# Gated cross-attention and expert layer on one core: scores on array quarters, and five reorderings of the work around them

## The chip, the cores and the metric

The kernel runs on one core of a Trainium2 chip. TensorE multiplies matrices into PSUM, VectorE (DVE), ScalarE (ACT) and GpSimd (POOL) do the rest, SyncE (SP) issues most transfers. The metric is the time of one execution in device microseconds. Before the change it is 368.51 us, the median of 6 runs that lie between 365.48 and 370.79.

## The reference, cut to what matters

All is float32. 8 sequences of 256 tokens with 128 features; the context has 1601 positions, of which the causal mask lets only the first 256 be seen. 16 heads of 64. Then each token goes through one of 8 experts (128 to 512 to 128).

```python
def attention(queries, keys, values, mask, Wq, bq, Wk, bk, Wv, bv, Wo, bo):
    q, k, v = ...                                    # 16 heads of 64
    scores = einsum('bhqd,bhkd->bhqk', q, k) / sqrt(64)
    scores = where(mask[:, None, None, :], -1e30, scores)
    scores = where(triu(ones((256, 1601)), k=1), -1e30, scores)
    out = softmax(scores) @ v
    return out @ Wo + bo

def experts(x, W1, b1, W2, b2, Wr, br):
    indices = argmax(softmax(x @ Wr + br))
    out = 0
    for i in range(8):                               # b1, b2 are added for every token
        mask = (indices == i)[..., None]
        h = relu((x * mask) @ W1[i] + b1[i])
        out = out + (h @ W2[i] + b2[i])
    return out

x = x + tanh(g_xattn) * attention(layernorm(x), ctx, ctx, mask, ...)
x = x + tanh(g_ffn) * experts(layernorm(x), ...)
```

A token whose visible keys are all masked attends to all 1601 positions alike; the kernel carries this case by a separate mean over the context (`ksum`, `mean_value`) and a weight `umask`. An expert that a token doesn't choose still adds `relu(b1) @ W2 + b2`; the sum of these over the experts is `total`.

## The kernel before, in words

Sequences are taken in 4 pairs (`p`), heads in 8 pairs (`c`); one turn of the main loop is one `g = 8 p + c`, 32 turns. The order on every engine is that of the program text (`manual_schedule`), so an instruction that waits holds all that stands behind it on its engine.

In turn `g` the text has, in this order: `turn(old, 0..3)`, which transposes the normalized probabilities of turn `old = g - 2` on TensorE and copies them to SBUF on VectorE (`probT`, two PSUM buffers), with `query(g + 1)`, `key(g + 1)`, `value(g + 2)` and the second half of the exps of turn `g - 1` between them; `normalized(g - 1)`, in which VectorE takes reciprocals and GpSimd multiplies the probabilities by them; work for other pairs (`beside_copies`, `beside_values`, `beside_scores`: normalization, transposes, output projection `y`, router); then `biases(g)` and `scores(g, b)` with `exps(g, 0)`, and `values(old)`. `query`, `key`, `value`, `values`, `y` and small products share the two PSUM buffers of `misc`.

`biases` writes mask and causal mask of the first 128 queries (t = 0) into the score banks by a bf16 product with the identity, 4 matmuls of 128x128 by 130 columns. `scores` adds the products of t = 0 (128 keys) and writes those of t = 1 (256 keys), for the two heads j = 0, 1 of the pair: K = 64 rows, so j sits in the upper or lower row half of the array. VectorE takes the maxima, for t = 1 together with the mask. Each bank tile `banks[b]` has one PSUM bank for each j.

Beside this, GpSimd issues five accumulating 1 MB loads and a short one (`add_keys`, L148 and L150) at the end of turns 0 to 5, each into the same tile; `join_keys` (L351) adds the halves of it at the end of turn 7; `mean_value` on TensorE begins with `cm_ps` (L357) after the scores of turn 8. `other(e)` and `others()` (turns 12 to 25) prepare the experts' constant, with a long VectorE sum (L335). `keep_weights` writes the experts' weights and constants to DRAM (`later`).

Tokens are routed by rows of 264 numbers that go to their expert's place in a DRAM tile `store` (`scatter`, an indirect transfer that GpSimd issues). `last_turns` does the last two head pairs' remaining work by halves of the last pair (`a`, `b`), plans on VectorE which chunks of 128 rows are already full (`plan_full`, 18 small steps), and fetches five of those (`fetch_full`: for each a number loaded to a register on SP, then the rows, then weights from `later`). `last_routing` runs these five chunks (`turned_rows`, `first_layer`, `second_layer`) while the last tokens are routed, and `experts()` the rest.

The start: loads, constants, `ln_stats` of pair 0 with its scales on GpSimd, warming matmuls (`keep_awake`), transposes, `query(0)`, `key(0)`, `mask_bias(0)`, `value(0)`, `value(1)`, routing constants, the mask biases of pairs 1 to 3, and then the loop.

Of the kernel before, what the change touches and what calls it, by code (L numbers as in the profile page):

```python
# [17 lines left out]
P = 128  # L18
B, S, D = 8, 256, 128
SK = 1601  # L20
# [21 lines left out]


# [5 lines left out]
def tile_gated_xattn_moe(  # L49
# [41 lines left out]
    def load_x(eng, p):  # L91
        eng.dma_start(
            out=x_sb[p].rearrange("p (b t) d -> p b t d", b=2),
            in_=x[2 * p : 2 * p + 2].rearrange("b (t p) d -> p b t d", p=P),
        )
# [28 lines left out]
    nc.sync.dma_start(out=mask_sb, in_=mask[:, 0:S].partition_broadcast(P))  # L124
    nc.sync.dma_start(out=wv_sb, in_=wv)

# [42 lines left out]
    causal = const.tile([P, SW], F32, name="causal")  # L169
    nc.gpsimd.memset(causal, 0.0)  # L170
    for at in (K0, K1 + P):
        nc.gpsimd.affine_select(
            out=causal[:, at : at + P],
            in_=causal[:, at : at + P],
            compare_op=ALU.is_ge,
            fill=NEG,
            base=0,
            pattern=[[-1, P]],
            channel_multiplier=1,
        )  # L180
# [5 lines left out]
    bias = const.tile([P, B, SW], BF16, name="bias")  # L186
# [14 lines left out]
    def plain_constants():  # L201
# [10 lines left out]
        nc.vector.memset(bias[:, :, 0:1], 0.0)  # L212
        nc.vector.memset(bias[:, :, U0 : U0 + 1], NEG_ALL)

        for b in range(2):
            nc.vector.memset(banks[b][:, :, U1 : U1 + 1], -NEG_ALL)

    def mask_bias(p):

        for at, n in ((K0, P), (K1, S)):  # L220
            nc.vector.scalar_tensor_tensor(
                out=bias[:, 2 * p : 2 * p + 2, at : at + n],
                in0=mask_sb[:, 2 * p : 2 * p + 2, 0:n],
                scalar=NEG,
                in1=causal[:, at : at + n].unsqueeze(1).to_broadcast([P, 2, n]),
# [46 lines left out]
    token_i, _ = counted("token", [NT], [[P, NT]], 0, 1)  # L272
# [3 lines left out]
    def routing_constants():  # L276
        nc.gpsimd.memset(before, 1.0)
# [3 lines left out]
        for i, f, pattern, base, mult in made:  # L281
            nc.gpsimd.iota(i, pattern=pattern, base=base, channel_multiplier=mult)
            nc.vector.tensor_copy(f, i)
        nc.vector.tensor_copy(rows[:, :, 2 * D : 2 * D + 1].bitcast(I32), token_i.unsqueeze(2))
# [8 lines left out]
    def experts_weights():  # L293

        nc.gpsimd.memset(blank, 0.0)
# [27 lines left out]
    def others():  # L323

        part = ws[:, :, FF + AT_C : FF + AT_C + D]
        zero = p1.tile([P, E, D], F32, tag="rest", name="zero")
        for h in range(2):
# [647 lines left out]
    def last_turns():  # L975
# [19 lines left out]
        for n in (10, 11):  # L995
            scatter(n)
            apart()
# [291 lines left out]
```

## Time and profile before

| | us |
|---|---|
| profiled execution, its own time | 367.18 |
| its span, first to last instruction | 365.5 |
| first score matmul (turn 0) | 18.45 |
| start of scores, turns 7, 8, 9 | 74.03, 81.57, 94.61 |
| start of scores, turns 20, 21, 22, 23 | 190.90, 202.81, 212.71, 220.39 |
| start of scores, turn 31 | 288.18 |
| first layer of the first chunk that `experts()` runs | 324.40 |

The groups of instructions by line, with shapes kept apart, show TensorE's parts; the columns are the busy time in us, the mean duration of one in ns, and the idle time just before them with what ended it:

```profile
L540 PE MATMUL pt<-ident,prob 128*128 128x128 f32 x384 | 63.9, 278 | 3.2 <-DVE probT L542 1.7 <-POOL prob L532 1.5
L478 PE MATMUL sc<-kT,qT 64*128 64x256 f32 x256 | 38.5, 377 | 0.0
L553 PE MATMUL o<-probT,v 128*64 128x256 f32 x240 | 37.6, 392 | 0.0
L478 PE MATMUL sc<-kT,qT 64*128 64x128 f32 x256 | 28.1, 296 | 0.0
```

An f32 matmul of the text is two instructions. The mean of one holds the way through the array, so rates are read from the starts in the timeline and not from it. `64*128` is the tile of the array: 64 rows, 128 columns.

The page's slices of the span (40 of 9.1 us) show the granted clock and the transfers:

```profile
PEclk9999999999999999999999999999999999899997
DMA  6999777768499994000000000057000016659930
```

The clock is full but for one place near 314 us and the end. SP's issues of the five early chunks in the tail:

```profile
302.06 2.10 SPq L876 DMA_DIRECT2D rows<-store  x2
304.48 0.33 SPq L886 DMA_DIRECT2D arena<-later  x1
305.65 1.46 SPq L876 DMA_DIRECT2D rows<-store  x2
307.35 0.33 SPq L886 DMA_DIRECT2D arena<-later  x1
308.53 0.34 SPq L876 DMA_DIRECT2D rows<-store  x1
309.10 1.66 SPq L886 DMA_DIRECT2D arena<-later  x3
```

### The profile page before, as it was taken

The page shows a single profiled execution, that of the slowest core. Times are in us where ns is not written, and L with a number is a line of the kernel's source. Part 1 is how long each engine was busy: PE and PEld are TensorE (multiplying, and loading weights), DVE is VectorE, ACT ScalarE, POOL GpSimd, SP SyncE. Part 2 cuts the span into 40 slices and gives each one's busy share as a digit, 9 for nine tenths or more (in the row PEclk, how much of TensorE's full clock was granted, in tenths as well). Part 3 has the DMA queues.
Part 4 walks back from the last instruction along what each step waited for, and adds up shares of the span by engine and source line. Part 5 has one row for each costly group of instructions (what it writes and reads, how often), then busy time and mean ns, then how long its engine had stood idle before and what let it go on. Part 6 is the DMA issues. An engine that isn't in the chain of part 4 may idle for free.

```text
span 365.5 us, 7926 instructions
## 1 busy us (share of the span) xinstructions
PE 342.6 (94%) x2598; PEld 246.0 (67%) x2598; DVE 241.5 (66%) x838; ACT 207.8 (57%) x743; POOL 214.5 (59%) x306
## 2 busy tenths in 40 slices
PE   8879999899999999999999899999999898689993
PEld 3345656467677776667775566777767686689993
DVE  3747777675667676786767877766667985354441
ACT  2567687563555758655575386555485532356651
POOL 4065765572456576769772567692666774417673
PEclk9999999999999999999999999999999999899997
DMA  6999777768499994000000000057000016659930
GB/s 196 288 144 208 108 115 116 169 235 227 131 388 387 383 384 169 2 2 2 3 0 17 15 16 18 2 224 311 7 24 19 0 61 189 257 157 330 406 145 13
DMA packets 36320, 53.58 MB, mean 147 GB/s; under 512 B 3801, under 2 KB 22829, under 8 KB 36280
## 3 DMA queue, kind: packets, MB, share of 16 engines
q1 hardware_dynamic: 28280, 44.07, 35.2%
q0 software_dynamic: 7360, 8.73, 12.6%
q8 instruction: 20, 0.33, 0.4%
q10 hardware_dynamic: 640, 0.29, 0.3%
q14 instruction: 20, 0.16, 0.1%
HBM read 27.82 MB, written 25.71 MB: 146 GB/s over the span
## 4 chain that ended last, share of the span: by engine, by line
PE 74%; DVE 9%; ACT 9%; issue 3%; DMA 2%; POOL 1%; POOLq 0%; SPq 0%; DVEq 0%; ACTq 0%
PE sc L478 11%; PE o L553 10%; PE pt L540 9%; PE q L438 6%; ACT prob L509 6%; PE y L592 6%; PE k L445 5%; PE hs L917 5%; PE v L456 5%; PE ys L933 5%; DVE sc L488 3%; PE y_last L710 2%; PE sc L467 2%; ACT kT L447 2%; DMA rows<-store 1%
## 5 line engine op out<-in xcount | busy, mean ns | idle before, releaser
L509 ACT ACTIVATE prob<-sc,nmax 128x129 f32<-128x129 f32 (+1 forms) x256 | 105.3, 426 | 92.2 <-DVE nmax L488 92.2
L532 POOL TENSOR_TENSOR prob<-prob,rs 128x256 f32<-128x256 f32 (+1 forms) x128 | 102.7, 861 | 63.5 <-DVE rs L523 63.3
L540 PEld LDWEIGHTS pt<-ident,prob 128*128 128x128 f32 x384 | 46.8, 141 | 54.4 <-issue 47.3
L542 DVE COPY probT<-pt 128x384 f32<-128x384 f32 x128 | 67.2, 545 | 16.3 <-PE pt L540 16.3
L540 PE MATMUL pt<-ident,prob 128*128 128x128 f32 x384 | 63.9, 278 | 3.2 <-DVE probT L542 1.7
L488 DVE CUSTOM_DVE_ANT_0 sc<-sc,bias 128x256 f32<-128x256 f32 x128 | 55.3, 432 | 4.4
L509 ACT ACTIVATION_READ_ACCUMULATOR prob<-sc,nmax 128x1 f32 x256 | 53.6, 209 | 0.0
L478 PE MATMUL sc<-kT,qT 64*128 64x128 f32 (+1 forms) x512 | 50.6, 337 | 0.0
L553 PE MATMUL o<-probT,v 128*64 128x256 f32 x480 | 45.6, 332 | 0.0
L553 PEld LDWEIGHTS o<-probT,v 128*64 128x64 f32 x480 | 29.7, 136 | 18.3 <-issue 8.0
L478 PEld LDWEIGHTS sc<-kT,qT 64*128 64x128 f32 x512 | 36.3, 187 | 4.9
L486 DVE TENSOR_REDUCE nmax<-sc 128x2 f32<-128x258 f32 x64 | 27.0, 422 | 12.3 <-PE sc L478 12.2
L438 PE MATMUL q<-xT,arena 128*128 128x512 f32 x64 | 33.2, 600 | 1.5 <-DVE xT L410 0.8
L456 PE MATMUL v<-arena,cT 128*128 128x512 f32 x64 | 33.0, 599 | 1.6 <-ACT qT L440 1.5
L445 PE MATMUL k<-cT,arena 128*128 128x512 f32 x64 | 33.5, 605 | 0.8 <-DVE total L336 0.8
L440 ACT ACTIVATE qT<-q,bqT 128x512 f32<-128x512 f32 x32 | 22.0, 688 | 13.9 <-PE q L438 13.1
L523 DVE RECIPROCAL rs<-ssum 128x4 f32<-128x4 f32 x64 | 11.0, 173 | 27.9 <-ACT prob L509 23.0
L951 POOL DMA_INDIRECT out_dram<-o,rows x18 | 17.9, 996 | 16.1 <-DMA rows<-store 8.3
L925 ACT ACTIVATE h<-hs,arena 128x128 f32<-128x128 f32 x60 | 17.2, 368 | 16.0 <-ACT h L925 8.8
L447 ACT ACTIVATE kT<-k,bT 128x512 f32<-128x512 f32 x32 | 22.2, 694 | 2.8 <-PE k L445 2.8
L569 DVE TENSOR_SCALAR arena<-o,bT 128x512 f32<-128x512 f32 x30 | 22.4, 746 | 1.2 <-PE o L553 1.2
L592 PE MATMUL y<-wo_sb,arena 128*128 128x128 f32 x192 | 23.1, 275 | 0.0
(234 smaller groups left out, 503.6 us busy)
## 6 DMA issues: line engine op xcount, KB each, us to landing
store<-blank SPq DMA_DIRECT2D x16, 1056.0 KB, 14.7
arena<-later SPq DMA_DIRECT2D x15, 578.0 KB
rows<-in_ctx_dram POOLq DMA_DIRECT2D x5, 1024.0 KB, 9.0
later<-ws SPq DMA_DIRECT2D x1, 4624.0 KB
rows<-store SPq DMA_DIRECT2D x23, 132.0 KB, 3.6
ws<-in_L_ffn_W_dram SPq DMA_DIRECT2D x1, 2048.0 KB
ws<-in_L_ffn_W_dram SPq DMA_DIRECT2D x8, 256.0 KB, 5.3
x<-in_x_dram SPq DMA_DIRECT2D x4, 256.0 KB
```

The lines of the kernel that those rows point to most:

```text
L438: nc.tensor.matmul(ps, lhsT=wq_sb[:, c * P : (c + 1) * P], rhs=xT[p], start=True, stop=True)
L445: nc.tensor.matmul(ps, lhsT=wk_sb[:, c * P : (c + 1) * P], rhs=cT[p], start=True, stop=True)
L447: nc.scalar.activation(kT[g], ps, AF.Identity, bias=bT[:, NC + c : NC + c + 1])
L456: nc.tensor.matmul(ps, lhsT=cT[p][:, t * P : (t + 1) * P], rhs=wv_sb[:, c * P : c * P + 512], start=True, stop=True)
L478: nc.tensor.matmul(s[:, j, at : at + n], lhsT=q[r, b * S + t * P : b * S + (t + 1) * P], rhs=k[r, b * S : b * S + n], start=(t == 1), stop ...
L488: nc.vector.tensor_tensor_reduce(out=s[:, j, K1:U1], in0=s[:, j, K1:U1], in1=bias[:, 2 * (g // NC) + b, K1:U1], scale=-1.0, scalar=-NEG_AL ...
L509: nc.scalar.activation(pr[:, j, lo:hi], s[:, j, lo:hi], AF.Exp, bias=m[:, t, j : j + 1], scale=-1.0 if t else 1.0, accum_out=sm[:, t, j : ...
L532: nc.gpsimd.tensor_tensor(pr[:, :, lo:hi], pr[:, :, lo:hi], r, ALU.mult)
L540: nc.tensor.transpose(ps[:, n * P : (n + 1) * P], pr[:, j, K0 + n * P : K0 + (n + 1) * P], ident)
L542: nc.vector.tensor_copy(pt, ps[:, 0 : 3 * P])
L553: nc.tensor.matmul(o[DK * j : DK * (j + 1), n * P : S], lhsT=v[:, 2 * b + n, cols], rhs=probT[g, 2 * b + j][:, 0:S] if n == 0 else probT[g ...
L592: nc.tensor.matmul(ps[:, i * D : (i + 1) * D], lhsT=attT[p * NC + c][:, t * P : (t + 1) * P], rhs=wo_sb[:, c], start=(c == 0), stop=(c == ...
```

## The change

Scores: queries of t = 1 are loaded with their two halves of 64 swapped, so that every matmul of `scores` and `biases` is 64 rows by 64 columns of the array (j selects the rows, u the columns), with only as many keys as the 64 queries of a quarter can see: 64, 128 for t = 0 and 256, 192 for t = 1. The mask tiles are built for that order; a token's number follows its row. GpSimd: layer norm scales of the next pair, `add_keys`, `add_bo`, `join_keys` and the experts' fills now stand behind `normalized` of a turn; `blank` is set at the start. The sum `total` is taken in four pieces, in eleven steps of `others()` instead of six. The first biases and scores stand ahead of the routing constants and of the second turn's projections. `router(2)`, `router_places(2)` and the scatters of the third pair stand a turn earlier, four of the first half's output products stand in turn 31, and the plan and `fetch_full` earlier in `last_turns`, with other weights between the rows.

```diff
+HB = P // 2
+BLOCK = ((0, 1), (3, 2))
...
     def load_x(eng, p):
-        eng.dma_start(
-            out=x_sb[p].rearrange("p (b t) d -> p b t d", b=2),
-            in_=x[2 * p : 2 * p + 2].rearrange("b (t p) d -> p b t d", p=P),
-        )
+        for at, t, lo in ((slice(0, P), 0, 0), (slice(0, HB), 1, P + HB), (slice(HB, P), 1, P)):
+            eng.dma_start(
+                out=x_sb[p][at, t::2],
+                in_=x[2 * p : 2 * p + 2, lo : lo + at.stop - at.start].rearrange("b q d -> q b d"),
+            )
...
     def mask_bias(p):
-        for at, n in ((K0, P), (K1, S)):
+        b = slice(2 * p, 2 * p + 2)
+        for part, out, keys, lo in (
+            (slice(0, P), bias0[0][:, b, K0:], causal0[0], 0),
+            (slice(0, P), bias0[1][:, b, K0:], causal0[1], 0),
+            (slice(0, P), bias[:, b, 0 : 3 * HB], causal1[:, 0 : 3 * HB], 0),
+            (slice(0, HB), bias[:, b, 3 * HB : S], causal1[:, 3 * HB : S], 3 * HB),
+        ):
...
     def routing_constants():
+        nc.gpsimd.memset(blank, 0.0)
...
+    def routing_casts():
...
     def experts_weights():
-        nc.gpsimd.memset(blank, 0.0)
...
         for h in range(2):
             ps = misc(f"zero_{h}")
...
-        yield
+            yield
+        for k in range(0, D, 32):
+            nc.vector.tensor_reduce(
+                total[:, k : k + 32], zero[:, :, k : k + 32].rearrange("p e d -> p d e"), AX.X, ALU.add
+            )
+            yield
...
-        nc.vector.tensor_reduce(total, zero.rearrange("p e d -> p d e"), AX.X, ALU.add)
...
     def biases(g):
         for b in range(2):
-            for j in range(2):
-                nc.tensor.matmul(
-                    banks[b][:, j, 0:K1], lhsT=ident_bf, rhs=bias[:, 2 * (g // NC) + b, 0:K1], start=True, stop=False
-                )
+            for u, keys in enumerate(bias0):
+                for j in range(2):
+                    r = slice(HB * j, HB * (j + 1))
+                    nc.tensor.matmul(
+                        banks[b][HB * u : HB * (u + 1), j, 0 : keys.shape[-1]],
+                        lhsT=ident_bf[r, r],
+                        rhs=keys[r, 2 * (g // NC) + b],
+                        start=True,
+                        stop=False,
+                    )
     def scores(g, b):
-        for at, n, t in ((K0, P, 0), (K1, S, 1)):
-            for j in range(2):
-                r = slice(DK * j, DK * (j + 1))
-                nc.tensor.matmul(
-                    s[:, j, at : at + n],
-                    lhsT=q[r, b * S + t * P : b * S + (t + 1) * P],
-                    rhs=k[r, b * S : b * S + n],
...
+        for t, at in enumerate((K0, K1)):
+            for u in range(2):
+                n = HB * (BLOCK[t][u] + 1)
+                for j in range(2):
+                    r = slice(DK * j, DK * (j + 1))
+                    lo = b * S + t * P + HB * u
+                    nc.tensor.matmul(
+                        s[HB * u : HB * (u + 1), j, at : at + n],
+                        lhsT=q[r, lo : lo + HB],
+                        rhs=k[r, b * S : b * S + n],
...
     def fetch_full():
-        weights_behind = {1: (0,), 3: (1,), 4: (2, 3, 4)}
+        weights_behind = {1: (0,), 4: (1, 2, 3, 4)}
...
-    def last_turns():
+    def last_turns(a):
-        scatter(8)
         normalized(l, 0)
+        plan(4)
         turn(g, 0)
         turn(g, 1)
         exps(l, 1)
-        scatter(9)
+        scatter(10)
         normalized(l, 1)
-        for n in (10, 11):
-            scatter(n)
-            apart()
+        scatter(11)
+        apart()
         a.residual()
-        a.out(*range(NC - 3))
-        plan(4)
+        a.out(NC - 4)
+        plan(5)
         turn(l, 0)
         turn(l, 1)
         a.attend(g, nc.scalar)
-        plan(5)
+        plan(len(steps))
+        fetch_full()
         a.out(NC - 3)
         turn(g, 2)
         turn(g, 3)
         a.attend(l, nc.scalar)
-        plan(len(steps))
-        fetch_full()
         a.out(NC - 2)
+        b.out(0)
         b.residual()
-        b.out(0)
...
         value(0)
         value(1)
+        biases(0)
+        scores(0, 0)
+        exps(0, 0)
+        scores(0, 1)
         routing_constants()
-        more_constants()
...
                 turn(old, 1)
+            if g == NG - 1:
+                o_old = misc(f"o_{old}")
+                a = Half(0, misc("y_last0")[:, 0:S], banks[0][:, 0, 0:S], banks[1][:, 0])
+                a.out(*range(NC - 4))
...
                     normalized(g - 1, b)
+            if 1 <= g < SK // S:
+                add_keys(g)
+            if g == SK // S - 1:
+                experts_weights()
+            if p + 1 < NPAIR and c == 3:
+                ln_scales(f"x{p + 1}")
+            if p < NPAIR and c == 4:
+                add_bo(p)
+            if g == NC:
+                join_keys()
+            if 2 * NC + 5 <= g < 2 * NC + 8:
+                next(rest_of)
...
-            if g < NG:
+            if g == 0:
+                beside_copies(p, c)
+                routing_casts()
+                more_constants()
+            if g > 0:
                 biases(g)
                 scores(g, 0)
...
             if g == NC:
                 next(mean)
             if old is not None:
-                values(old)
-            if g < SK // S:
+                values(old, o_old if g == NG - 1 else None)
+            if g == NG - 3:
+                router(2)
+            if g == 0:
                 add_keys(g)
-            if g == SK // S - 1:
-                experts_weights()
             if NC + 4 <= g < NC + 4 + E:
                 other(g - NC - 4)
-            if NC + 4 + E <= g < NC + 10 + E:
+            if NC + 4 + E <= g < NC + 12 + E:
                 next(rest_of)
-            if g == NC + 11 + E:
+            if g == NC + 12 + E:
                 keep_weights()
-            if p < NPAIR and c == 3:
-                add_bo(p)
-            if g == NC - 1:
-                join_keys()
             if 20 <= g < 24:
                 scatter(g - 20)
-            if 26 <= g < 30:
-                scatter(g - 22)
             if g == NG - 2:
                 residual(NPAIR - 1)
+            if 26 <= g:
+                scatter(g - 22)
```

## The prediction

> **What bounds the kernel now.** I read the page first: the busy row, then the chain of waits by engine.
>
> ```profile
> PE 342.6 (94%) x2598; PEld 246.0 (67%) x2598; DVE 241.5 (66%) x838; ACT 207.8 (57%) x743; POOL 214.5 (59%) x306
> ...
> PE 74%; DVE 9%; ACT 9%; issue 3%; DMA 2%; POOL 1%; POOLq 0%; SPq 0%; DVEq 0%; ACTq 0%
> ```
>
> TensorE is the path; the rest of it is a few stalls. Next the timeline of TensorE in one plain turn of the loop (a turn is one `g`).
>
> ```profile
> 217.24 1.03 PE L445 MATMUL k<-cT,arena 128*128 128x512 f32 x2
> 218.11 0.49 PE L540 MATMUL pt<-ident,prob 128*128 128x128 f32 x3
> 218.44 1.02 PE L456 MATMUL v<-arena,cT 128*128 128x512 f32 x2
> 219.30 0.49 PE L540 MATMUL pt<-ident,prob 128*128 128x128 f32 x3
> 219.63 0.60 PE L409 MATMUL tr_y<-ident,rows 128*128 128x128 f32 x4
> 220.06 0.39 PE L467 MATMUL sc<-bias,ident_bf 128*128 128x130 bf16 x4
> 220.39 1.58 PE L478 MATMUL sc<-kT,qT 64*128 64x128 f32 x16
> 221.90 1.52 PE L553 MATMUL o<-probT,v 128*64 128x256 f32 x16
> ```
>
> Starts follow each other without a hole: biases 0.33 us, scores 1.51, values 1.45. `k` streams 2 x 512 columns in 0.87 us, so an f32 matmul instruction costs 0.85 ns a column. The 16 score instructions hold 8x128 + 8x256 = 3072 columns, 2.61 us in single file; they take 1.51. So two row halves (j = 0, 1) already run side by side, at 1.31 us, and 0.20 us is the first weight load and the change of tile shape. Score to score is 7.6 to 7.7 us in such a turn, 9.0 to 9.5 where an output projection (`y`) stands in it.
>
> Then the three places where TensorE waits or will wait: GpSimd in turns 5 to 8, VectorE's long sum in turn 22, and the tail.
>
> ```profile
> 65.85 1.34 POOL L150 DMA_DIRECT2D rows<-in_ctx_dram  x1 [4.46 <-DMA rows<-in_ctx_dram]
> 66.69 1.05 POOL L295 MEMSET blank<- 128x528 f32 x1
> 67.80 0.13 POOL L298 MEMSET blank<- 128x1 int32 x2
> 67.90 3.16 POOL L532 TENSOR_TENSOR prob<-prob,rs 128x256 f32<-128x256 f32 x4
> 73.19 3.16 POOL L532 TENSOR_TENSOR prob<-prob,rs 128x256 f32<-128x256 f32 x4 [2.13 <-DVE rs L523]
> 76.31 2.35 POOL L351 TENSOR_TENSOR rows<-rows 128x1024 f32<-128x1024 f32 x1
> 80.75 3.16 POOL L532 TENSOR_TENSOR prob<-prob,rs 128x256 f32<-128x256 f32 x4 [2.08 <-DVE rs L523]
> ```
>
> ```profile
> 83.08 1.95 PE L357 MATMUL cm_ps<-ones,rows 128*128 128x1 f32 x16
> ```
>
> ```profile
> 207.33 1.91 DVE L335 TENSOR_REDUCE total<-zero 128x128 f32<-128x1024 f32 x1
> ```
>
> ```profile
> 313.54 0.33 PE L908 MATMUL xs<-ident,rows 128*128 128x128 f32 x1 [3.29 <-DMA rows<-store]
> 313.70 1.69 PE L917 MATMUL hs<-xsT,arena 128*128 128x128 f32 x8
> 315.37 2.05 PE L933 MATMUL ys<-arena,h 128*128 128x128 f32 x8
> 317.22 1.13 PE L917 MATMUL hs<-xsT,arena 128*128 128x128 f32 x8
> 318.18 1.06 PE L933 MATMUL ys<-arena,h 128*128 128x128 f32 x8
> ```
>
> **Scores on quarters, the largest term.** A row half streams 2 x (128+256) = 768 columns a turn, twice. In quarters, u=0 gets 64+256 and u=1 gets 128+192, so each quarter streams 640. If four run side by side: 2 x 640 x 0.85 = 1.09 us for 1.31, -0.22. Of the 0.20 us overhead, the first load has 64 columns instead of 128 (-0.05), and biases and scores share one shape, so the change of shape comes before the biases and not between. Biases: 8 matmuls for 4. Now the four cost 4 x 0.056 = 0.22 and the rest of their 0.33 is that change. With four at once there are two rounds of 0.06: -0.1; one after another +0.24. I take the first, since the row pairs start together. Sum: -0.35 us a turn; bounds -0.45 (all overhead shared) and +0.6 (only two quarters at once: 2 x 1280 columns, 2.18 us for 1.31, less 0.25 of the other savings).
>
> [...] The row: 16 one-column f32 matmuls on 128-column weights (`cm_ps`) take 1.95 us, 0.11 a load, so a plain 64-column load is 0.057 us; 14 bf16 ones (L648 to L652, 287.51 to 287.86) take 0.025 each. [...]
>
> ScalarE has its own loop: scores, VectorE's maxima, 4.6 us of exps with qT and kT between them, then the biases of b=1 (in turn 28 it starts 2.56 us after the scores and ends at 273.3, for biases at 273.4). It shortens too, because the biases and scores of b=0 lie in it (about 1.0 us, then 0.6), so it caps nothing above -0.35.
>
> **Where turns 1 to 6 lose it.** GpSimd's five accumulating loads each wait for the one before (9.2 us apart, 18.20 to 65.85), longer than a turn, and their order against `normalized` is unchanged. So turn 7 hangs on 65.85, whatever was gained before. What does change there: the 1.05 us memset of `blank` moves to the start, hidden in GpSimd's idle 8.36 us before 18.20; turn 7 comes 1.0 earlier. `add_bo(0)` (1.3 to 1.9 us) moves ahead of `normalized(4)` and uses up that one's slack of about 1.7 us in turn 6. So: -1.0 for turns 1 to 7, not 6 x -0.35. Extra DMA issues on SP (three for one per `load_x`, 0.45 us each) can push the first accumulating load by up to 0.9.
>
> **Start.** First scores begin 2.9 us earlier (15.5 for 18.45: qT and kT are ready at 14.1). But ScalarE must still do v, v, exps, qT, kT, v, qT, exps, kT before the next biases: from nmax at 17.8 that is 1.6 + 5.1 + stalls of 0.4 = 24.9, for 25.4 now; two extra `x` issues (0.45 each) take that back. 0 (-0.6 to +1.0), and turn 7 swallows it. VectorE's mask biases for pairs 1 to 3 (2.90 us now, some 0.3 more a pair in four pieces) and the routing casts (0.75 us now, two small ones more) move behind the first maxima; VectorE has 2.3 us idle before those now and 2.7 after, so nothing waits for them before the maxima of turn 1 at 26.8. If that cover fails, 1 us, swallowed likewise.
>
> **`join_keys` moves behind `normalized(7)`: a new wait.** Now it runs at 76.31 to 78.66, in idle time. Afterwards GpSimd does `normalized(7)` first (80.75 to 83.91), then the join to 86.26. `cm_ps` needs it at 83.08, and TensorE's whole queue (values, turn 9) stands behind: +3.2 us, paid in full, as turn 9 is dense. An idle of 3.29 us in the tail was followed by matmuls at half speed (1.69 and 2.05 for 1.13 and 1.06, 1.55 us lost). [...] I take no clock loss and keep 1.55 in the range.
>
> **Other GpSimd moves at nothing.** `ln_scales` of the next pair (four instructions, 1.8 us) goes behind `normalized`; its reader `xn` stands a turn later. `add_keys` keeps its neighbours. `add_bo` of later pairs lies in turns with 3 us of GpSimd idle. Without that cover each costs up to its own 1.3 to 1.9 us.
>
> **The long sum.** Turn 22 takes 9.90 us between score starts (202.81 to 212.71) where its like, turn 14, takes 7.68; of the 2.2, 0.48 is `all_ps`, the rest VectorE's 1.91 us before the probT copies. Pieces of about 0.5 fit the 0.5 to 0.6 us that VectorE has before each copy is missed. -1.7 (-1.0 to -2.1). Weights are kept a turn later, 240.83 to about 257, and first read at 304: hidden.
>
> **Routing early and the tail.** `a.out(0..3)`, 16 instructions of 0.112 = 1.8 us, go into turn 31's hole of 1.46 us, but wait for `o_28`'s eviction at 286.14, so turn 31 grows by about 0.8 net of `router_places` (0.35) leaving it. The next transposes still wait for GpSimd (6.3 us after the scores), so nothing returns there. Row fetches: SP issues them at 302.06 to 308.53, 1.35 us after the plan (300.71). The plan's VectorE steps move up by about 1.2 us less the 0.8; and the second weight load (578 KB) no longer precedes the fifth fetch, which goes out 1.3 us earlier with a shorter queue ahead of it. So its 3.29 us wait mostly goes. What is late next is the second weight load, about 312 for 312.9, then first layers at full clock (1.55 saved). -2.6 in all, including the 0.8 (bounds -5, all of wait and clock, and +0.8, none).
>
> **Sum.** Turns 7, 8 and 9 to 31 are 25: 25 x -0.35 = -8.75. With -1.0, +3.2, -1.7 and -2.6: -10.85. The profiled execution took 367.18 (span 365.5); it becomes 356.3. It lies 1.3 under the median of 368.51, so I forecast 357.7.
>
> **Rivals.**
> 1. Quarters advance in step: each group lasts as long as its widest member, 128 and 256 columns as now, and only overhead goes, -0.15 a turn. 25 x +0.20 = +5.0: 362.7. For it: no unequal widths run side by side in this trace. Against: nothing in the row pairs shows a common barrier. Chance 0.2.
> 2. Slower: only two of four quarters run at once. +0.6 for -0.35 in 25 turns is +23.75: 381. The other terms sum to -2.1, so the kernel is slower once biases and scores together grow by more than 2.1 / 25 = 0.08 us a turn, that is with scores over about 1.7. Against: halves by rows (scores) and by columns (values, 16 in 1.45 us) each run in pairs, and a quarter is the crossing of both. Chance 0.12.
> 3. The join's wait isn't there or is small because GpSimd is done earlier: 357.7 - 3.2 = 354.5. Chance 0.1.
> 4. The edit doesn't do what it says in the tail: weights still hold the rows up, +2.6: 360.3. Chance 0.1.
>
> The forecast itself has 0.48. Range 351 to 366: rivals 1, 3 and 4 with the term bounds, rival 2 left out. A measurement here tells about 1% from no change. Faster by over 1% (under 364.8): 0.78; within 1%: 0.10; slower: 0.12.
>
> **What would show it.** Scores from about 1.51 to 1.25 us a turn between their first start and that of the values, or 1.3 and more (rival 1), or 2 (rival 2). GpSimd's join after 83 and TensorE idle about 3 us before `cm_ps`. No 1.9 us reduce; turn 22 near 7.5. `xs` waiting under 1 us and no half-speed stretch near 314. Turn 7's start moving by only 1 to 1.5 us. I am wrong in kind if turns of 9 us do not shrink, or if VectorE or GpSimd ends TensorE's waits in plain turns.

## The result and the profile after

The kernel after takes 370.05 us (median of 36 runs, 368.14 to 376.92), the one before 367.59 in the same comparison (78 runs, 364.0 to 371.12): ratio 1.0074, 95% interval 1.006 to 1.0088. So it is slower by 0.7%, where the forecast was 357.7. The profiled execution took 369.49 us (span 367.8), 2.31 more than the one of before. First the busy row, the granted clock and the chain of waits by engine, from the page of after.

```profile
PE 338.2 (92%) x3238; PEld 238.7 (65%) x3238; DVE 245.1 (67%) x857; ACT 207.3 (56%) x743; POOL 216.3 (59%) x315
...
PEclk9999999996799999999999999999999989999998
...
PE 60%; DVE 17%; ACT 8%; DMA 5%; issue 4%; POOL 4%; POOLq 0%; SPq 0%; DVEq 0%; ACTq 0%
```

TensorE is busy 4.4 us less in a longer span, its share of the chain fell from 74% to 60%, VectorE's rose from 9% to 17%, and the clock has a dent near 87 us. The dent, in the timelines of GpSimd and TensorE around turns 8 and 9 (start, busy, engine, line, operation, count, and in brackets the idle time before with what ended it):

```profile
81.18 3.17 POOL L586 TENSOR_TENSOR prob<-prob,rs 128x256 f32<-128x256 f32 x4 [4.07 <-DVE rs L577]
84.30 2.34 POOL L392 TENSOR_TENSOR rows<-rows 128x1024 f32<-128x1024 f32 x1
```

```profile
81.74 1.31 PE L532 MATMUL sc<-kT,qT 64*64 64x64 f32 x32
86.69 3.57 PE L398 MATMUL cm_ps<-ones,rows 128*128 128x1 f32 x16 [3.64 <-POOL rows L392]
90.20 2.83 PE L607 MATMUL o<-probT,v 128*64 128x256 f32 x16
92.95 0.90 PE L594 MATMUL pt<-ident,prob 128*128 128x128 f32 x3
93.65 1.91 PE L482 MATMUL q<-xT,arena 128*128 128x512 f32 x2
```

`join_keys` (L392) follows `normalized(7)` as forecast and `cm_ps` waits 3.64 us. What was not forecast stands below it: `cm_ps` takes 3.57 us for 1.95, `o` 2.83 for 1.52, `q` 1.91 for 1.02. A table by stretches has half the clock, 0.50, up to 95.4. Its columns are the length of the stretch, the busy time of TensorE, weight loads, VectorE, ScalarE and GpSimd (instructions in brackets), the granted clock, the share of the transfer engines and GB/s:

```profile
86.60:95.40 8.80, 8.71 (x38) 6.57 (x39) 1.48 (x3) 0.00 (x0) 0.29 (x3) 0.50 0.43 110
```

The start of scores in each turn divides the 2.31 us. All numbers are us, from the two timelines, and for the kernel with the quarters alone (below) from its own:

| stretch | before | quarters alone | after | after less before |
|---|---|---|---|---|
| start of scores in turn 7 | 74.03 | 76.61 | 74.60 | +0.57 |
| turn 9 | 13.04 | 12.63 | 20.60 | +7.56 |
| a plain turn (10 to 13) | 9.02, 9.46 | 8.73, 9.17 | 8.73, 9.17 | -0.29 each |
| turns 14, 28 | 7.68, 7.61 | 7.65, 7.57 | 7.64, 7.58 | -0.04, -0.03 |
| turns 21 to 24 together | 38.06 | 37.21 | 37.06 | -1.00 |
| turns 30, 31 | 7.72, 6.73 | 7.48, 6.71 | 8.54, 6.40 | +0.82, -0.33 |
| all turns 8 to 31 | 214.15 | 208.85 | 217.43 | +3.28 |
| last scores to the end | 77.29 | 81.85 | 75.75 | -1.54 |

The periods of turns 8 to 31 repeat within 0.03 us from execution to execution of the same order of work, but for turn 31 (6.71 and 6.58 with quarters alone, in two kernels) and turn 9, which is told at the end. The start and the tail move far more: with the order of before, turn 7 starts at 73.4 to 74.0 and the tail takes 77.3 to 83.5 us; with that of after, 74.6 to 76.1 and 75.7 to 82.8. So the first and the last row of the table hold for this pair of profiles only. In the five groups of experiments below the kernel before took 371.84, 375.5, 367.56, 367.72 and 366.36 us, so ratios to it are compared between groups, and microseconds only within a profile's turns.

### The profile page after: what moved, and what is told of

It is laid out like the page before. It is cut to its first block, busy times and chain, and to the rows that moved or that the text cites. A ratio compares the mean times of both kernels' runs of the same rounds, so it can differ in the third digit from the quotient of the medians.

```text
span 367.8 us, 9250 instructions
## 1 busy us (share of the span) xinstructions
PE 338.2 (92%) x3238; PEld 238.7 (65%) x3238; DVE 245.1 (67%) x857; ACT 207.3 (56%) x743; POOL 216.3 (59%) x315
## 3 DMA queue, kind: packets, MB, share of 16 engines
q0 software_dynamic: 7360, 8.73, 12.6%
## 4 chain that ended last, share of the span: by engine, by line
PE 60%; DVE 17%; ACT 8%; DMA 5%; issue 4%; POOL 4%; POOLq 0%; SPq 0%; DVEq 0%; ACTq 0%
PE pt L594 8%; DVE sc L542 6%; PE k L489 6%; PE o L607 6%; PE y L646 6%; PE hs L972 5%; PE sc L532 5%; PE q L482 5%; PE v L500 5%; ACT prob L563 5%; PE ys L988 4%; DVE nmax L540 3%; DMA rows<-in_ctx_dram 3%; PE y_last L765 2%; DVE arena L623 2%
## 5 line engine op out<-in xcount | busy, mean ns | idle before, releaser
L594 PE MATMUL pt<-ident,prob 128*128 128x128 f32 x384 | 65.5, 282 | 7.5 <-POOL prob L586 4.5
L607 PE MATMUL o<-probT,v 128*64 128x256 f32 x480 | 46.9, 339 | 0.0
L532 PE MATMUL sc<-kT,qT 64*64 64x256 f32 (+3 forms) x1024 | 42.0, 298 | 0.0
L489 PE MATMUL k<-cT,arena 128*128 128x512 f32 x64 | 35.1, 630 | 1.9 <-DVE arena L623 1.6
L482 PE MATMUL q<-xT,arena 128*128 128x512 f32 x64 | 34.2, 616 | 2.0 <-DVE arena L623 1.1
L532 PEld LDWEIGHTS sc<-kT,qT 64*64 64x64 f32 x1024 | 31.5, 134 | 0.1
```

The costliest lines, as they stand in the source:

```text
L482: nc.tensor.matmul(ps, lhsT=wq_sb[:, c * P : (c + 1) * P], rhs=xT[p], start=True, stop=True)
L489: nc.tensor.matmul(ps, lhsT=wk_sb[:, c * P : (c + 1) * P], rhs=cT[p], start=True, stop=True)
L532: nc.tensor.matmul(s[HB * u : HB * (u + 1), j, at : at + n], lhsT=q[r, lo : lo + HB], rhs=k[r, b * S : b * S + n], start=(t == 1), stop=True,)
L594: nc.tensor.transpose(ps[:, n * P : (n + 1) * P], pr[:, j, K0 + n * P : K0 + (n + 1) * P], ident)
L607: nc.tensor.matmul(o[DK * j : DK * (j + 1), n * P : S], lhsT=v[:, 2 * b + n, cols], rhs=probT[g, 2 * b + j][:, 0:S] if n == 0 else probT[g ...
```

## The experiments

**The join.** One line back at the end of turn 7 in the kernel after, and the same line moved the other way in the kernel before:

```diff
-            if g == NC:
-                join_keys()
...
+            if g == NC - 1:
+                join_keys()
```

> The kernel after, with join_keys alone put back at the end of turn 7. Theory (the join behind normalized(7) holds cm_ps up by 3.6 us and the idle halves the clock for some 7 us): the period of turn 9 goes from 20.6 to 12.7 us, all other turns stay within 0.3, and the time falls by 7.5 to 8 us, to about 362.3. Rival (the join is only one of several late things there, such as the zb chain or the second bank of scores): turn 9 keeps 2 to 4 us of it and the time falls by 4 to 5, to about 365.5.

Measured: 0.986 (0.9812 to 0.9908) of before, so 2.1% under after; turn 9 is 12.63 and every other turn from 8 on as in after.

> The kernel before with join_keys alone moved behind normalized(7). Theory: turn 9 goes from 13.0 to 20 to 21 us as in after, the time rises by 7 to 7.6, to about 375. As forecast (the wait of 3.2 us without a loss of clock): about 370.8.

Measured: 1.0204 (1.0155 to 1.0253), and turn 9 at 19.16 us for 13.04. The move alone costs 7.4 us by the times (5.8 to 9.4 by the interval) and 6.1 by its turn, which is less than expected here but far from the 3.2 that were forecast. `cm_ps` waits 3.11 us, near the forecast; the slow stretch behind it (granted clock 0.50, 85.60 to 91.9) lasts 6.3 us for the 8.7 in after, and half of it, 3.15, is about the 3.0 that the turn lost beyond the wait. Then the wait was left and only the idle filled, with `keep_awake(14)` ahead of `cm_ps`:

> The kernel after with 14 bf16 matmuls of 512 columns (0.21 us each, 3.0 us, into a spare PSUM slot, read by nobody) ahead of cm_ps in turn 8; the join stays behind normalized(7). Theory (the 3.64 us of idle cost 3.6 us of waiting and, by the halved clock after them, about 4.2 more): cm_ps waits under 1 us behind the filler and its successors run at full clock, turn 9 takes 16 to 16.5 us for 20.6, ratio to before about 0.996 (1.0074 less 4.2 us of 370). Rival (turn 9's other 4 us are waits of their own, not clock): turn 9 stays at 20 or more, ratio 1.007.

Measured: turn 9 takes 16.34 us for 20.60, ratio 1.0008 (0.9979 to 1.0037). The timeline of TensorE in that kernel:

```profile
83.41 3.22 PE L212 MATMUL awake<-ones_bf 128*128 128x512 bf16 x13
87.11 1.95 PE L398 MATMUL cm_ps<-ones,rows 128*128 128x1 f32 x16 [0.48 <-POOL rows L392]
88.99 1.52 PE L607 MATMUL o<-probT,v 128*64 128x256 f32 x16
...
90.83 1.02 PE L482 MATMUL q<-xT,arena 128*128 128x512 f32 x2
```

`cm_ps` starts as late after the scores as in after (4.94 us), but what follows runs at full speed (`o` 1.52, `q` 1.02). Of the 7.97 us that turn 9 grew against the quarters alone, 4.26 were the clock and 3.71 the wait. The time fell by less than turn 9 did: 0.7%, by the two intervals at most 1.0%, for 1.2%, and the expected ratio of 0.996 lies below the interval. The two ratios come from different groups, and start and tail move by more than this between groups; where the rest went is not shown.

**GpSimd's other moves.** The kernel after with `join_keys`, `ln_scales` of the next pair and `add_bo` back, the second behind `ln_stats` and the third at the end of its turn:

```diff
-            if p + 1 < NPAIR and c == 3:
-                ln_scales(f"x{p + 1}")
-            if p < NPAIR and c == 4:
-                add_bo(p)
...
+            if c == 3:
+                ln_scales(f"x{n}")
...
+            if p < NPAIR and c == 3:
+                add_bo(p)
```

> The kernel after, with join_keys, ln_scales of the next pair and add_bo all at their places of before (add_keys and the blank memset stay as in after). Theory (turns 5 and 6 lost 1.8 us each because ln_scales and add_bo stand between add_keys and normalized, but turn 7 hangs on the chain of accumulating loads anyway): turns 5 and 6 fall back to 7.6 to 8 us, turn 7 grows to 9 or more, and beyond the join only 0.5 to 1.3 us come off: about 361.5. Rival (the loads do not cap it): all 3.6 us come off beyond the join, about 358.7.

Measured: 0.9892 (0.9835 to 0.995), no better than the join alone. Turns 5 and 6 take 8.14 and 7.74 us (9.44 and 9.41 in after, 7.43 and 8.91 with the join alone), turn 7 takes 8.82 (8.03, 7.67), and scores of turn 7 start at 75.62, with the join alone at 75.75. The kernels with the order of after up to turn 7 take 7.43 to 9.44 in turn 5, 8.26 to 9.41 in turn 6 and 7.66 to 8.14 in turn 7, so turn 5 tells nothing; turn 6 is shorter here and turn 7 longer than in any of them. As in the theory, where these moves stand shifts time between turns and not turn 7's start, which hangs on the loads.

**The quarters.** On the kernel before, with nothing else of the change:

> The kernel before with the quarters alone (x rows permuted, the four pieces of the masks, biases and scores on quarters, token numbers). Theory (four quarters advance at once and each plain turn from 9 to 31 gains 0.29 us, turns before 7 nothing): 367.6 - 6.5 = about 361 (359.5 to 362.5). Rival (a quarter's gain is eaten elsewhere once the other parts are away, as in turns 14, 17, 18 and 23 to 28 of after): 364 to 366. Second rival (quarters in step): scores to values 1.43 us, 365.

Measured: 0.9973 (0.994 to 1.0006), some 1 us; the expected 361 was wrong. Turns 8 to 31 gain 5.30 us, near to what was said, and the start loses 2.58 in the profile, or 3.25 against `b_join_late` of the same group, whose text up to turn 7 is that of before. Its timeline of TensorE in turn 7:

```profile
69.72 0.33 PE L580 MATMUL pt<-ident,prob 128*128 128x128 f32 x1 [1.69 <-POOL prob L572]
70.72 0.44 PE L580 MATMUL pt<-ident,prob 128*128 128x128 f32 x2 [0.67 <-POOL prob L572]
70.99 1.56 PE L468 MATMUL q<-xT,arena 128*128 128x512 f32 x2
72.34 0.85 PE L580 MATMUL pt<-ident,prob 128*128 128x128 f32 x3
72.98 1.91 PE L475 MATMUL k<-cT,arena 128*128 128x512 f32 x2
```

Before, the waits here were 0.85 and 0.66 and `q` and `k` took 1.02 each. The last load of the chain is issued 1.16 us later than before (67.01 for 65.85), and with it the multiply that these transposes wait for; TensorE's own work is only 0.34 later (`o` at 66.52 for 66.18). So it waits 0.84 longer, and the work behind the wait takes longer too: 0.54 more for `q`, 0.36 for the three transposes (0.85 for 0.49), 0.89 for `k`. `k`'s 1.91 and the transposes' 0.85 are near what two matmuls of 512 columns (`q`, 1.91) and three transposes (0.90) take in after at the granted clock of 0.50.

Whether quarters go in step was asked by leaving the rows in their own order, where the quarters of the second block see 192 and 256 keys:

```diff
-BLOCK = ((0, 1), (3, 2))
+BLOCK = ((0, 1), (2, 3))
```

`load_x` and the token numbers are those of before, the masks match.

> The kernel before with quarters on rows in their own order: the two quarters of the second block see 192 and 256 keys (u=0 sums 256 columns, u=1 384) where the change has 256 and 192, so that x is loaded in one DMA as before and token numbers stay. Theory (quarters advance each on its own, and the x loads cost the start 2 to 3 us): scores to values take 1.35 us for 1.24, a plain turn gains 0.18, the start loses nothing, ratio about 0.988. Rival (quarters go in step, widest member): scores to values 1.24 as in the change, ratio 0.982. Second rival (the start is lost to the masks or biases, not to the loads): 0.995 or more.

> The quarters on rows in their own order once more, for a profile that is undisturbed in the start. By the theory of the split x loads, the second accumulating load starts at 28 to 28.8 us, since x is loaded in one piece; by the rival at 29.5 to 31. Turns from 8 on as in its first run (plain turns 0.19 under before's).

Measured: scores to values 1.45 us in both, a plain turn 0.19 under before; ratio 0.9902 (0.9858 to 0.9946). That ratio rests on four of the ten times, which spread from 368.78 to 378.47 (their median 375.08, before 375.5), and the second run took 368.83 us once (before 367.72), so the time is not settled by them; the periods are. The 1.35 of the expectation was worked out without the two instructions of each f32 matmul: u=1 streams 2 x 64 columns more than in the change, 2 x 128 x 0.85 ns = 0.22 us, 1.46. In step, the widest member is 128 and then 256 columns in both kernels, and both would take the same. 1.24 and 1.45 show that each quarter goes on its own.

**Where the quarters' gain stops.** Turns 10 to 13, 15, 19 to 21, 23, 27 and 29 gain 0.26 to 0.30; turns 14, 22 and 28 gain 0.03 to 0.05. TensorE's own part shrinks by more. Turn 23 of the quarters alone, to be laid beside the rows of before in the prediction:

```profile
215.56 0.49 PE L580 MATMUL pt<-ident,prob 128*128 128x128 f32 x3
215.92 1.12 PE L475 MATMUL k<-cT,arena 128*128 128x512 f32 x2
216.88 0.49 PE L580 MATMUL pt<-ident,prob 128*128 128x128 f32 x3
...
218.39 0.60 PE L439 MATMUL tr_y<-ident,rows 128*128 128x128 f32 x4
...
219.02 1.31 PE L518 MATMUL sc<-kT,qT 64*64 64x64 f32 x31
220.25 1.52 PE L593 MATMUL o<-probT,v 128*64 128x256 f32 x16
```

From `tr_y` over the biases to the first scores (219.01) it is 0.62 us, before 0.76; from there to the values 1.24, before 1.51. That is 0.41, and every turn from 8 to 31 has such a gain, 0.40 to 0.52, 10.3 us in all. But the turn gains only 0.28, for 0.13 goes back at `k`, which stands 0.36 behind its transposes for 0.32 and takes 0.96 to the next start for 0.87. VectorE's copy of `o` out of PSUM, which frees the buffer that `k` writes, before and then with quarters:

```profile
216.35 0.74 DVE L569 TENSOR_SCALAR arena<-o,bT 128x512 f32<-128x512 f32 x1
```

```profile
215.11 0.75 DVE L609 TENSOR_SCALAR arena<-o,bT 128x512 f32<-128x512 f32 x1
```

Before, it ended at 217.09, 0.15 us ahead of `k`; now it ends at 215.86 and `k` starts at 215.92, at once. So VectorE's queue sets `k` even in a plain turn. Over turns 8 to 31 the steps at `k` take 3.9 us of the 10.3 back, half of it in turns 14, 17, 18, 25, 26 and 28 (0.29 to 0.41 each); another 0.4 is lost in turn 22, behind VectorE's long sum. The timelines of TensorE and of VectorE in turn 14 of the quarters alone (of TensorE's rows and VectorE's maxima, only the first and the last):

```profile
133.44 1.52 PE L593 MATMUL o<-probT,v 128*64 128x256 f32 x16
134.89 0.55 PE L580 MATMUL pt<-ident,prob 128*128 128x128 f32 x3
...
137.01 1.12 PE L475 MATMUL k<-cT,arena 128*128 128x512 f32 x2 [0.38 <-DVE arena L609]
```

```profile
133.57 0.39 DVE L526 TENSOR_REDUCE nmax<-sc 128x2 f32<-128x258 f32 x1
...
135.85 0.43 DVE L528 CUSTOM_DVE_ANT_0 sc<-sc,bias 128x256 f32<-128x256 f32 x1
136.21 0.14 DVE L528 DVE_READ_ACCUMULATOR2_ANT nmax<- 128x1 f32 x1
136.21 0.74 DVE L609 TENSOR_SCALAR arena<-o,bT 128x512 f32<-128x512 f32 x1
```

`o` is complete at about 134.9, but VectorE evicts it at 136.21, behind all maxima, and `k` needs its PSUM buffer. Moving the eviction between the maxima of b=0 and b=1 tests this (on the best kernel below, which was run again beside it; `scores_of` is the matmuls of `scores`, `maxima` the rest):

```diff
+                early = 2 <= g < NG - 1
+                (scores_of if early else scores)(g, 1)
...
                 values(old, o_old if g == NG - 1 else None)
+            if g > 0 and early:
+                maxima(g, 1)
```

> The kernel after with the join back, b2's sum early, router(2) back and the mask biases ahead of the first scores, and in turns 2 to 30 VectorE's maxima of b=1 behind the eviction of o (attT) and no longer ahead of it. Theory (in turns 14, 22 and 28 the quarters' gain ends in k's wait of 0.3 to 0.4 us for the PSUM slot of o, whose eviction is queued on VectorE behind all maxima): no such wait is left, those turns fall from 7.6 to 7.4 us, turns 17, 18, 25 and 26 by up to 0.15, the time by 1 to 1.5 us against the same kernel without it. Rival (the maxima of b=1, 1 us later, hold up the exps): turns grow by 0.3 to 1 us.

> The same without the early eviction, once more and in more rounds, as the measure for it and for a version that beats both kernels: ratio to before 0.980 to 0.985, turns 14, 22 and 28 at 7.6 us.

Measured: 0.9957 (0.9933 to 0.9982) against 0.9864 (0.9822 to 0.9906) for its base. Turns 14 and 28 fall from 7.64 and 7.57 to 7.50 and 7.44 and `k` no longer waits, but the plain turns grow by 0.28 against the base. The rows of turn 14:

```profile
137.35 1.02 PE L490 MATMUL k<-cT,arena 128*128 128x512 f32 x2
138.59 0.52 PE L602 MATMUL pt<-ident,prob 128*128 128x128 f32 x3 [0.21 <-DVE probT L604]
```

So the cause is confirmed, in the plain turns too (`k` stands 0.33 behind its transposes and takes 1.02 again), and the cure falls: the next transposes now wait for VectorE's probT copies, which stand behind the later maxima. In neither of the two orders does VectorE have room in this part of a turn.

**The start.** GpSimd's chain of key loads begins its second load at 27.9 to 28.8 us in the kernels that load x in one piece and keep whole scores, and at 28.9 to 31.6 in all others. First, the first load of the chain earlier on SP's queue:

```diff
+    nc.sync.dma_start(out=ksum, in_=keys_at(SK - TAIL - S))
     load_x(nc.sync, 1)
     load_c(nc.sync, 1)
-    nc.sync.dma_start(out=ksum, in_=keys_at(SK - TAIL - S))
```

> The kernel before with the first load of keys (ksum) issued ahead of the loads of x and c of pair 1, and nothing else. Theory (the start up to turn 7 hangs on the chain of six loads of keys, and its first issue sets it): GpSimd's accumulating loads each start 1.5 to 2 us earlier, turn 7 likewise, and the time falls by as much, ratio about 0.995. Rival (something else holds turns 3 to 7): ratio 1.00 with the chain earlier.

> The quarters alone on the kernel before, with ksum issued ahead of x and c of pair 1. Theory (three issues for one in each load of x put ksum 2 us later, and the longer wait that follows at turn 7 halved the clock): against the quarters alone the chain starts 3 to 4 us earlier, turn 7 gains 3 to 4.5 us, ratio to before 0.986 to 0.99. Rival (the quarters lost their gain in the start for another reason): 0.997 as without it.

Measured: 1.0009 (0.997 to 1.0049) and 0.9942 (0.99 to 0.9984). GpSimd's first load starts at 15.57 and 17.62, earlier by some 1.7 or more, and the second at 27.90 and 29.48, as without. The theory that the first issue sets the chain falls. Then the loads of x alone, in three pieces, on the kernel before:

> The kernel before with each load of x in three pieces (as many issues and bytes as in the change, rows in their old order), and nothing else. Theory (the split x loads alone set the chain of key loads back): GpSimd's second accumulating load starts at 29.5 to 31 us, as in every kernel with the change's x loads, instead of 27.9 to 28.8, and turn 7 starts 1 to 2 us later than before's 73.2 to 74.0; ratio 1.003 to 1.005. Rival (the masks, biases or the clock of the quarters do it): second load at 28 to 28.8, ratio 1.000.

Measured: 1.0048 (1.0014 to 1.0083), turn 7 at 76.36. The issues of GpSimd in that kernel:

```profile
19.62 1.86 POOL L149 DMA_DIRECT2D rows<-in_ctx_dram  x1 [9.39 <-DMA rows<-in_ctx_dram]
...
30.82 1.59 POOL L149 DMA_DIRECT2D rows<-in_ctx_dram  x1 [0.35 <-DMA rows<-in_ctx_dram]
```

Two issues more for each load of x cost 1.8 us (0.5 to 3.1). But `b_quarters_plain2`, with x in one piece, has its second load at 30.95 after a first at 17.46, so this is not the only cause. The two last trials, each on the kernel with the join back, b2 early and `router(2)` back (see below):

> The kernel after with the join back, b2's sum early, router(2) back, and x and c of pairs 2 and 3 loaded only once the second accumulating load has been issued (0.984 without this last part). Theory (in the first 30 us the queue's loads and the first accumulating load share the transfer engines): the second accumulating load starts 1.5 to 3 us earlier, at 27 to 29 us, turn 7 by 1 to 2 us, ratio 0.979 to 0.981. Rival (the first accumulating load is slow for another reason, its descriptors on GpSimd for one): no change, 0.984.

> The same base (join back, b2 early, router back; 0.984) with the mask biases of pairs 1 to 3 ahead of the first scores again, as in before, so that VectorE's 3.7 us of them no longer run while the first accumulating load is being made. Theory of this collision: the first accumulating load takes 10.6 us for 11.3 to 12.7, the second starts 1 to 2 us earlier, GpSimd's two copies behind it take 0.18 us for 0.9 to 1.2, ratio 0.979 to 0.982. Rival (no collision, the transfers set it): second load at 30 us as in the base, first scores 3 us later, ratio 0.984 to 0.987.

Measured: 0.9842 (0.9799 to 0.9885) with the second load at 29.57, and 0.9813 (0.976 to 0.9866) with it at 30.00; 0.9841 without either, so neither is a gain clear of noise. In the first the load no longer waits for a transfer: it follows GpSimd's own multiplies of `normalized(0)`, from 28.02 to 29.6, at once. In the second, GpSimd's two small copies take 0.18 us again, for 0.94 and 0.88 in after and 1.51 and 2.44 in `a_router_back`, where VectorE's mask biases ran beside them; the chain doesn't care. Why the first accumulating load takes 10.6 to 10.7 us to the next issue in some kernels and 11.2 to 13.7 in others stays open.

**The long sum.** The product of b2 made in turn 3 (`router_constants`) and kept in SBUF as `b2_all`, with the join back:

```diff
-        all_ps = misc("all_ps")
-        nc.tensor.matmul(all_ps[:, 0:D], lhsT=ones[0:E, :], rhs=b2_sb, start=True, stop=True)
-        nc.vector.tensor_tensor(total, all_ps[:, 0:D], total, ALU.add)
+        nc.vector.tensor_tensor(total, b2_all, total, ALU.add)
```

> The kernel after with join_keys back in turn 7 and the sum of b2 (all_ps) made in turn 3 into SBUF, so that the long sum's last addition needs no PSUM slot. Theory (in turn 24 q waits 1.1 us for the slot that all_ps pushed on to o's eviction, which gave most of the long sum's gain back): turn 24 falls from 9.92 to 8.34 us, turns 21 to 23 stay, 1.5 us beyond the 0.986 of the join alone: about 0.982. Rival (VectorE's extra pieces hold turn 24): it stays above 9.3.

Measured: turn 24 takes 8.73 us for 9.92 (8.34 was expected; what holds the other 0.39 is not shown), ratio 0.9836 (0.9772 to 0.9901), by the times not to be told from the join alone. The timeline of TensorE in turn 24 of after shows what was taken away:

```profile
224.47 1.52 PE L607 MATMUL o<-probT,v 128*64 128x256 f32 x16
225.93 0.48 PE L376 MATMUL all_ps<-b_sb,ones 8*128 8x128 f32 x2
226.34 0.55 PE L594 MATMUL pt<-ident,prob 128*128 128x128 f32 x3
227.99 1.13 PE L482 MATMUL q<-xT,arena 128*128 128x512 f32 x2 [1.10 <-DVE arena L623]
```

`all_ps` takes the second of two buffers behind `o`, so `q` must wait for the eviction of `o`, which stands behind the maxima.

**The tail.** On this base (the join back, b2 early), `router(2)`, `router_places(2)` and the scatters behind them in their old turns; then the whole tail as before; then only the plan's first steps behind the probT copies:

```diff
         normalized(l, 0)
-        plan(4)
         turn(g, 0)
         turn(g, 1)
+        plan(4)
```

> The kernel with the join back and b2's sum early (0.9836 to before) with router(2) and router_places(2) back in turns 30 and 31 of their places of before, and the last scatters with them; all else of the tail as in after. Theory (router(2) at the end of turn 29 costs turn 30 one us on VectorE's probT copies): turn 30 falls from 8.53 to 7.5 us, turn 31 grows by under 0.5, the time falls by 0.5 to 1, ratio 0.981. Rival (the plan needs the routing a turn ahead, and the tail gives it back): the tail from the last scores grows by 1 us or more, ratio 0.984 or above.

> The same base with the whole tail as before (router, places, scatters, the order of the last turns, a.out in the tail, weights behind the fetches). Theory (the change's tail is worth about 1.2 us from the last scores on, and loses 0.75 in turns 30 and 31): turns 30 and 31 fall by 0.75 together, the tail grows by 1 to 2 us, ratio 0.984 to 0.987. Rival (what the tail gained in the profile was the chip's loads, not the order): ratio 0.981.

> The same base with the first four steps of the plan behind the probT copies of turn 30's probabilities (turn(g, 0), turn(g, 1)) and not ahead of them. Theory (VectorE's 2.0 us of plan steps hold the copies, TensorE idles 2.61 us and drops to a lower clock): that idle falls under 1 us, the stretch behind it runs at full clock, the plan ends no later, and the tail shortens by 1 to 2 us, ratio 0.979 to 0.981. Rival (the plan is the critical one): the row fetches start 1 us later and the time stays.

Measured, on one chip: 0.9841 (0.9783 to 0.9899), 0.9854 (0.9775 to 0.9933) and 0.9885 (0.9823 to 0.9947), not to be told apart by time. By turns: with `router(2)` back turn 30 falls from 8.54 to 7.48, turn 31 grows from 6.40 to 6.58, and the tail is 75.30 us for 75.72 in `a_awake`, whose tail is that of after; routing a turn earlier buys nothing. With the whole tail as before it is 77.54, and the wait of `xs` for rows is back at 2.61 us. With the plan behind the copies the wait of 2.61 us goes, one of 1.85 comes in a later place, and the tail is 75.60: no gain. On this chip, then, the change's tail is 1.8 us shorter than that of before.

## Why the prediction was wrong, point by point

The sum said -10.85 us, the profiles say +2.31. The 13.2 us between them, term by term; the step that turned the sign is the join:

- **Start, -1.35 forecast (with turn 7's own 0.35), +0.57 found.** That turn 7 hangs on the chain of loads was right. The issues of x were priced at up to 0.9 and left out of the sum; split x alone costs 1.8. Over the other profiles the start lost more, 74.6 to 76.1 for 73.4 to 74.0. The cover of `ln_scales` and `add_bo` ("moves at nothing") failed: they stand between a late load and `normalized` in turns 5 and 6, but the chain takes that back in turn 7.
- **Quarters, -8.4 forecast in turns 8 to 31 (24 x 0.35), -5.30 found.** On TensorE the mechanism was right and the gain larger than said: 1.24 us from scores to values where 1.25 was said, no lockstep, and 0.14 from the biases and the change of shape where 0.1 was said. One after another, the eight bias matmuls were put at 0.24 more; no turn shows that (`tr_y` to the first scores takes 0.62 us for 0.76). What failed is that the whole of it was to shorten the turn. The prediction gave as a sign of being wrong in kind that VectorE ends TensorE's waits in plain turns, and it does: its copy of `o` sets `k`, which takes 0.13 back in a plain turn and 0.4 in turns 14 and 28.
- **The join, +3.2 forecast, +7.97 found.** This is the step that failed. The place, the waiting instruction and the wait were right (3.64 us). The loss of clock behind it was put at none in the sum and at 1.55 in the range; it was 4.26. The forecast had the row for it, 3.29 us of idle followed by half speed, and took its cost from the few short matmuls that happened to stand there. Half the length of the slow stretch, which work filled (8.71 of 8.80 us, granted clock 0.50), comes near the price: 8.7 us from 86.69 to 95.4, so 4.35, for the 4.26 found. `b_join_late` agrees: 6.3 us, so 3.15, for 3.0 found. That a wait of 3.2 us leaves the clock alone was the author's choice, and it is not shown: a slow stretch followed 3.64 us of idle in after (granted clock 0.50), 3.29 in before (0.56 from 313.5 to 317.2), 3.11 in `b_join_late` (0.50) and 2.61 in the tail of after (0.51). The slow stretches of the two joins lasted 8.7 and 6.3, the first 3.5 of each one-column products. With 3.2 for the join, the other terms as found come to -2.46, so the sign would have been right.
- **The long sum, -1.7 forecast, -0.14 found.** The pieces did hide VectorE's reduce: turn 22 fell from 9.90 to 7.65. But `all_ps` kept its place behind `o` in a later turn and made a buffer late there, 1.58 us in turn 24 against the quarters alone, and 0.49 went in turns 21 and 23. With it out of the way turns 21 to 24 take 35.87 for 37.21, -1.34.
- **Routing and tail, -2.6 forecast, -0.79 found.** Turn 31 with its block of products was to grow by 0.8 and shrank by 0.31. `router(2)` at the end of turn 29 was given no price and costs turn 30 1.06. The wait of `xs` went as said, but the plan's earlier steps hold the probT copies, with TensorE's filler gone to turn 31: 2.61 us idle in a new place, with the clock at 0.51 behind it (300.8 to 304.0). The -1.54 of the tail is from this one pair of profiles; the group on one chip above has -1.8.

The sum of the found terms: 0.57 - 5.30 + 7.97 - 0.14 - 0.79 = 2.31. No rival covered it. Rival 2's sign was right by another mechanism; rivals 1 and 3 fall with the 1.24 us and the join at 84.30, rival 4 with the wait of `xs` that went.

**A faster kernel.** Quarters, with the join back in turn 7, b2's product in turn 3, `router(2)` in turn 30 and the mask biases ahead of the first scores: 0.9813 (0.976 to 0.9866) and, in the second group, 0.9864 (0.9822 to 0.9906) of before, so some 5 to 7 us under it, and under after.

## What to carry to other kernels

Price a new wait on TensorE with and without a slow stretch behind it, at the density of the work there: here 3.6 us of waiting became 8.0, with the clock at 0.50 for 8.7 us, and one line moved back was worth more than the whole new matmul form. Before counting a saving in each turn of a loop, name what each other engine still has queued when TensorE comes earlier: VectorE's eviction took a third of it in plain turns and nearly all of it in turns 14 and 28. A small product that takes a PSUM buffer between two large ones puts the next matmul on the eviction of the one before it (`q` waited 1.10 us for it in turn 24 of after); ask for each edit which buffer is handed on, and not only which engine is free.

## What the hardware showed that was not expected

- The clock fell without idle time just ahead of it. In the second run of the best kernel `cm_ps`, 16 matmuls of one column, ran right behind the scores at full speed (granted clock 1.00), and yet what followed ran at half (0.52 from 87.03 to 90.40):

```profile
85.15 1.95 PE L399 MATMUL cm_ps<-ones,rows 128*128 128x1 f32 x16
87.03 2.74 PE L608 MATMUL o<-probT,v 128*64 128x256 f32 x16
89.70 0.90 PE L595 MATMUL pt<-ident,prob 128*128 128x128 f32 x3
90.40 1.11 PE L483 MATMUL q<-xT,arena 128*128 128x512 f32 x2
```

  Turn 9 took 14.26 us there and in `a_late_loads`, 12.63 or 12.64 in the other kernels that have quarters in this order, the join in turn 7 and maxima ahead of the eviction. What made the clock fall is not shown.
- The length of a wait alone doesn't decide the clock behind it. The same wait of TensorE in the tail was followed by a clock of 0.50 in `a_join_back` (2.61 us, then 292.30 to 294.00) and by full clock in `a_gpsimd_back` (2.60 us, then 292.15 to 304).
- VectorE's small steps of the plan varied in length: `tri_full`, 64 numbers a partition, took 0.59 us before, 1.35 in after and 0.23 in `a_router_back`, in the last two with GpSimd's multiply beside it; there another step of 40 numbers, `wide_full`, took 1.70 (0.99 in after, 0.20 before), also beside that multiply. What decides which step is long stays open.
